# Attention's residual added by accumulating transfers, its bias by ScalarE; one more product in parts, and three jobs at other points of the slot

## The chip, the cores and the metric

The kernel runs on one core of one Trainium2 chip. The metric is the device time of one execution in microseconds (us). The core's engines are named as in the profile: PE (TensorE), DVE (VectorE), ACT (ScalarE), POOL (GpSimd, which also issues transfers) and SP (SyncE, which only issues transfers). Each engine works through its own queue in order.

## The reference

Two layers work on four images of 64 x 64 pixels with 256 channels. The first is full self-attention over the 4096 pixels of an image with a residual; the second is a depthwise 3 x 3 convolution ("perception"), two pointwise layers with a GELU, and a local attention over 3 x 3 windows.

```python
# layer 0, per image, N = 4096 pixels
q, k, v = x @ Wq + bq, x @ Wk + bk, x @ Wv + bv          # q, k: 32 wide; v: 256 wide
x = gamma * softmax(q @ k.T) @ v + x
# layer 1
perceived = depthwise_conv3x3(x, w_perc) + b_perc         # 256 -> 768 channels
hid = gelu(perceived @ w_up1 + b_up1)                     # 768 -> 512
h = x + hid @ w_up2 + b_up2                               # 512 -> 256
q, k, v = split(h @ w_qkv + b_qkv)
out = h + local_attention_3x3(q, k, v)
```

## The kernel before, in words

**Slots.** An image is cut into 8 blocks of 8 rows (512 pixels), so there are 32 slots (NSLOT). Slot s runs the attention of block s, and beside it the later work of earlier blocks: the perception of block s-2, the hidden layer, update, guide, scores and local values of block k = s-3, and the output of block a = s-5. The order of every engine is the order in which the program is written.

**Points.** A slot has 16 points. At point p, PE makes the energies of half group n = p+2 (two key tiles of 128 pixels; one tile `e` that all half groups share), the jobs of that point from the list `jobs`, and the weighted product of half group p (line 492). ACT turns `e` into the weights `p` by an exponential (line 434); there are three buffers of `p`. At the end of a slot stands DVE's summing up: the denominators (lines 528 to 562), and `evacuate` (line 579), which empties the four accumulators that the next slot's first product needs. At point 0 of the next slot `finish` scales the result (line 602).

**Products in parts.** A product in plain fp32 costs PE more than one whose operands were split into three parts (high, low, gap). ACT makes the high part (lines 439, 448), DVE the low and the gap (457/458 for one key tile, 522/532 for two). The even half groups are split whole. Of the odd ones only the second key tile is split, but both are in 9, 11 and 13 (`BOTH_IN_PARTS`). This is so in the "full" slots, which are all from 3 to 30 but 7, 15 and 23: 25 slots. `load_alone` (L346) loads the values' forms for this; the first tile's forms use the one buffer of `hid`.

**Denominators.** In a full slot the weights of half groups 0 to 13 (in the first slot of an image 2 to 13) are summed by transfers that POOL issues with accumulation (`sent<-p`, lines 509/511), and those of 14 and 15 by DVE. The send of half group n stands in the program at point n-1, ahead of that point's jobs. A buffer of `p` is free for half group n+3 only when the send of n has landed.

**The residual.** `xp` is a ring of four blocks of the input with a zero column on either side. `renew` loads a block at the start of its slot. `finish` adds attention's result and the bias to it by two DVE instructions (line 608), and `rim` (POOL) copies or clears the row that lies beyond the ring's end. Each block's perception reads one row of the block below: the taps with dy = 2, which are the 11th and later of its 54 DVE steps. `share` says how many steps stand behind each point.

**The jobs at the end of a slot.** `local_values` makes values of the local attention on PE (line 1036) and adds the bias on DVE (1048). `scores` has PE (1076), an exponential on ACT (1096) and a mask on POOL (1101). `local_sum` is eight POOL instructions (1120 to 1127; one more for a block on an image's edge). `border` is a short product (1017), an exponential and one or two POOL instructions. The two halves of `local_values` stand at points 10 and 13, the scores at 11 and 12, `local_sum` at 12 behind the second scores, `border` at 14.

Of the kernel before, what the change touches and what calls it, by code (L numbers as in the profile page):

```python
# [11 lines left out]
AF = mybir.ActivationFunctionType  # L12
ALU = mybir.AluOpType
# [4 lines left out]
B, H, W, C = 4, 64, 64, 256  # L18
N = H * W
CQK = C // 8  # L20
CH = C // P
HP, WP = H + 2, W + 2
NB = 512
RB = NB // W
# [15 lines left out]
NG = NT // GRP  # L40
SQ = 32
NJ = NB // SQ
NSLOT = B * NBLK
# [7 lines left out]
BELOW = 1.0 - 2.0**-13  # L51
IN_PARTS = (2, 4, 6, 8, 10, 12, 14)
ONE_IN_PARTS = (1, 3, 5, 7, 9, 11, 13, 15)
BOTH_IN_PARTS = (9, 11, 13)
BY_DMA = (3, 5, 7, 9, 11, 13)
BY_DMA_IF_FULL = tuple(range(14))

# [5 lines left out]
def attention_then_perception_kernel(  # L63
# [19 lines left out]
    nc = tc.nc  # L83
# [3 lines left out]
    def loaded(src, name, shape=None, queue=None):  # L87
        t = const.tile(list(shape or src.shape), F32, tag=name, name=name)
        (queue or nc.sync).dma_start(out=t, in_=src)
        return t  # L90
# [10 lines left out]
    def unshifted():  # L101
# [6 lines left out]
        def tile_of(shape, tag, name, bufs=1):  # L108
            return pool.tile(shape, F32, tag=tag, name=name, bufs=bufs)

        def bank(tag, name):
            return psum.tile([P, NB], F32, tag=tag, name=name, bufs=dict(m=2, acc=2 * CH)[tag])
# [14 lines left out]
        xv = xp.rearrange("p c (h w) -> p c h w", w=WP)  # L127

        def ring(slot):

            return 1 + slot % RING * RB
# [15 lines left out]
        for r in range(4):  # L147
            nc.scalar.dma_start(
                out=bqk2[r * CQK : (r + 1) * CQK, :], in_=b_qk[:, r % 2 : r % 2 + 1]
# [17 lines left out]
        for r in range(KR):  # L167
            m = near[r * KW : (r + 1) * KW]
            for half in range(2):

                for sign in (1, -1):
                    nc.gpsimd.affine_select(
                        out=m[:, half], in_=m[:, half], compare_op=ALU.is_ge, fill=0.0,
# [13 lines left out]
        for q in range(0, P, SQ):  # L187
            part = fold[q : q + SQ].rearrange("p (j r) -> p j r", r=SQ)
            nc.gpsimd.affine_select(
                out=part, in_=part, compare_op=ALU.not_equal, fill=1.0,  # L190
# [3 lines left out]
        def watch(values):  # L194

            n = values.free_size()
            for i in range(0, n, P):
                at = watched[:, : min(P, n - i)]
                nc.gpsimd.tensor_tensor(at, at, values[:, i : min(n, i + P)], ALU.add)
# [3 lines left out]
        def seen():  # L203

            i = next(free)
            return watched[:, i : i + 1]
# [15 lines left out]
        def full(s):  # L222
            return s > LAG_PERC and s % NBLK < NBLK - 1
# [7 lines left out]
        def alone(s, n):  # L231

            if last_one(s, n):
                return [1] * (n in ONE_IN_PARTS)
            return [i for i, ns in enumerate((BOTH_IN_PARTS, ONE_IN_PARTS)) if full(s) and n in ns]

# [116 lines left out]
        def project_v(s, pair, tag="m"):  # L353
# [10 lines left out]
            n = 2 * (s % NBLK) + pair  # L364
            split, one, both = (n in ns for ns in (IN_PARTS, ONE_IN_PARTS, BOTH_IN_PARTS))
            h = packed_h[:, s, bass.ts(pair, 2 * C)].rearrange("p (t c) -> p t c", c=C)
# [84 lines left out]
        def low_and_gap(s, n):  # L451
            for i in alone(s, n):
                high, (_, low, gap) = highs[s, n, i, P], rests.pop((s, n, i))
                if low is None:
                    low, gap = (tile_of([P, NB], "vs", f"o{x}_{s}_{n}", 4) for x in "lg")
                p = weights[s, n // 2, n % 2][:, i, :]
                nc.vector.tensor_tensor(low.bitcast(F32R), p, high, ALU.subtract)
                nc.vector.scalar_tensor_tensor(
                    gap.bitcast(F32R), low, -SPLIT, high, ALU.mult, ALU.add
                )  # L460
                lows[s, n, i, P], gaps[s, n, i, P] = low, gap
# [84 lines left out]
        def shared(s):  # L546

            a = s - LAG_ATT + 1
            return a if 0 <= a < DIRECT - 1 else None
# [15 lines left out]
        def on_all(values, turned, out, copy=nc.vector.tensor_copy):  # L565

            copy(
                squares(turned), values.unsqueeze(2).to_broadcast([P, NJ, SQ])
            )
            nc.vector.transpose(out, turned)  # L570

        def evacuate(s):
            acc = accs.pop(s)
            os = [tile_of([P, NB], "o", f"o_{s}_{c}", 2) for c in range(CH)]
            for o, gap in zip(os, acc[CH:]):
                nc.scalar.mul(o, gap, -1.0 / (SPLIT + 1.0))
            if in_two_sums(s):
                for c, o in enumerate(os):
                    nc.vector.tensor_tensor(o, acc[c], o, ALU.add)
                acc = os  # L580
            evacuated[s] = os, acc

        def finish(s, parts=((0, RB),)):

            n = NJ * (1 if shared(s) is None else 2)
            ps = bank("m", f"dps_{s}")[:, :n]
            given = parts_.pop(s).rearrange("p i j -> p (i j)")[:, :n]
            nc.tensor.matmul(ps, lhsT=fold, rhs=given, start=True, stop=True)
            inverse = tile_of([P, 2, NJ], "inverse", f"inverse_{s}")
            inverses[s] = inverse  # L590
            nc.vector.reciprocal(inverse.rearrange("p i j -> p (i j)")[:, :n], ps)

            rden = sums.pop(s)[:, 1, :]
            on_all(inverse[:, 0, :], turneds[s][:, 0, :], rden)
            watch(inverse.rearrange("p i j -> p (i j)")[:, :n])
            if s not in evacuated:
                evacuate(s)
            os, totals_ = evacuated.pop(s)
            for r0, r1 in parts:
                n = slice(r0 * W, r1 * W)  # L600
                for o, total in zip(os, totals_):
                    nc.vector.scalar_tensor_tensor(
                        o[:, n], total[:, n], gam_parts[:, 0:1], rden[:, n], ALU.mult, ALU.mult,
                        accum_out=seen(),
                    )
                for c, o in enumerate(os):
                    dst = xv[:, c, ring(s) + r0 : ring(s) + r1, 1 : 1 + W]
                    nc.vector.scalar_tensor_tensor(
                        dst, o[:, n].rearrange("p (h w) -> p h w", w=W), gbv[:, c : c + 1], dst,
                        ALU.add, ALU.add,  # L610
                    )
                if len(parts) > 1:
                    yield
            if s < NSLOT - 1:
                rim(s)
            yield

        def rim(s):


            g = s % NBLK
            if g == RING - 1:
                nc.gpsimd.tensor_copy(xv[:, :, 0, :], xv[:, :, RP - 2, :])
            elif g == NBLK - 1:
                nc.gpsimd.memset(xv[:, :, 0, :], 0.0)
            if g == RING:
                nc.gpsimd.tensor_copy(xv[:, :, RP - 1, :], xv[:, :, 1, :])
            elif (g == 0 and s > 0) or s == NSLOT - 2:
                nc.gpsimd.memset(xv[:, :, RP - 1, :], 0.0)
# [567 lines left out]
        def job(f, s, *args, n=NSLOT):  # L1197
            return [lambda: f(s, *args)] if 0 <= s < n else []
# [30 lines left out]
        for slot in range(NSLOT):  # L1229
            b, g = divmod(slot, NBLK)  # L1230
            if slot >= RING:
                renew(slot)
            k, a = slot - LAG_HID, slot - LAG_ATT
# [3 lines left out]
                job(hidden_part, k, 1, 0), job(hidden_part, k, 1, 1),  # L1237
                job(local_product, a, 0), job(local_product, a, 1),
                job(update, k, 0), job(update, k, 1), job(guide, k, 0),
                job(guide, k, 1), job(local_values, k, 0), job(scores, k, 0),  # L1240
                job(scores, k, 1) + job(local_sum, k - 1), job(local_values, k, 1),
                job(border, k), [],
            ]
            if slot in (1, 2):
                jobs[0] = [lambda: next(combine)] * 2
# [10 lines left out]
            n_steps, stepped = n_mixed, 0  # L1256


            share = [2, 6, 8, 4, 7, 2, 7, 4, 6, 4, 3, 1, 0, 0, 0, 0]
            if slot == LAG_PERC:  # L1260
                share = [4, 3, 6, 4, 5, 4, 5, 1, 5, 1, 5, 1, 5, 1, 4, 0]
            if slot == NSLOT - 1:
# [21 lines left out]
            for point in range(points):  # L1284
# [22 lines left out]
                    load_forms(*soon)  # L1307
                if point == 0:
                    low_and_gap(slot, 1)
                for do in jobs[point]:  # L1310
                    do()
                if slot and point == 0 and in_two_sums(slot - 1):
                    next(finish(slot - 1))
# [21 lines left out]
                if slot == 0 and point == 1:  # L1335
                    wb = const.tile([P, CH, MULT, TAPS + 1], F32, tag="wb", name="wb")
                    nc.gpsimd.dma_start(out=wb[:, :, :, :TAPS], in_=w_perc)
                    bias = loaded(b_perc, "bperc", queue=nc.gpsimd)
                    wperc, bperc = wb[:, :, :, :TAPS], wb[:, :, :, TAPS]
                    gam = loaded(gamma.partition_broadcast(P), "gam", [P, 1])  # L1340
                    gbv = loaded(b_v.rearrange("o (c p) -> p (o c)", p=P), "gbv")
# [33 lines left out]
            if in_two_sums(slot):  # L1375
                evacuate(slot)
            elif slot < NSLOT - 1:
                next(finish(slot))
# [17 lines left out]


        finishing = finish(last, ((0, 1), (1, RB)))
        next(finishing)
        run((guide, last - 2, 0, 0), (guide, last - 2, 1, 0))  # L1400
# [392 lines left out]
    with tc.manual_schedule():  # L1793
        wv, gam, wperc, bperc, wup1, bup1, wup2, bup2, blqk, blv = unshifted()
# [50 lines left out]
```

## Time and profile before

| | before |
|---|---|
| runs shown, median of 3 (lowest to highest) | 3191.09 us (3189.49 to 3192.02) |
| the profiled execution's own time | 3190.59 us |
| its span, first to last instruction | 3188.9 us |
| granted TensorE clock | 0.999 |
| PE busy | 3166.7 us, 99% |
| DVE busy | 2921.0 us, 92% |
| ACT busy | 1632.7 us, 51% |
| POOL busy | 745.4 us, 23% |
| DMA | 703.22 MB, 320504 packets |

Around the span lie 1.7 us. A "busy" PE may be waiting inside a matmul, since the ends of matmuls are modelled; starts are what the timeline is read by. Lines are named L and a number, tiles as in the program without their buffers' numbers, and `out<-in` says what an instruction writes and reads.

### The profile page before, as it was taken

Reading aid. Unit: us, or ns where it says so; the run is one execution under the profiler, and the core shown is the slowest. Engines: PE = TensorE matmul, PEld = TensorE weight load, DVE = VectorE, ACT = ScalarE, POOL = GpSimd, SP = SyncE. Lnnn points to the kernel's source line nnn. Section 1 sums busy time; section 2 is a strip of 40 time slices with the busy share of each in tenths; the row PEclk is TensorE's granted clock in tenths of the full one; section 3 lists DMA queues with packets and bytes.
Section 4 is the critical chain, followed back from the end, with each engine's and each line's share of the span. In section 5 each row is a group of like instructions: output and inputs, shape, how many; then the busy total and the mean of one; then the engine's idle time right before and its main releaser. Section 6 shows DMA issues by size and latency. Waiting matters only on the chain.

```text
span 3188.9 us, 39777 instructions
## 1 busy us (share of the span) xinstructions
PE 3166.7 (99%) x12652; PEld 2279.5 (71%) x12652; DVE 2921.0 (92%) x4264; ACT 1632.7 (51%) x2249; POOL 745.4 (23%) x1070
## 2 busy tenths in 40 slices
PE   9999999999999999999999999999999999999998
PEld 5557777766777777776777777777677777777755
DVE  5789999989999999998999999999899999999994
ACT  4445555555555555554555555554555555555432
POOL 4201122221222221222122222211221222222221
PEclk9999999999999999999999999999999999999999
DMA  8778888777888888877888888896788888888620
GB/s 269 227 206 220 231 225 232 226 235 230 228 232 244 238 223 241 227 205 249 239 223 234 225 243 236 229 239 194 260 232 232 223 232 228 240 238 239 165 51 28
DMA packets 320504, 703.22 MB, mean 221 GB/s; under 512 B 97233, under 2 KB 98273, under 8 KB 320161
## 3 DMA queue, kind: packets, MB, share of 16 engines
q1 hardware_dynamic: 246336, 448.01, 43.7%
q0 software_dynamic: 67280, 240.98, 34.2%
q10 hardware_dynamic: 6672, 11.60, 1.0%
q8 instruction: 105, 1.72, 0.2%
q14 instruction: 111, 0.90, 0.1%
HBM read 425.83 MB, written 79.82 MB: 159 GB/s over the span
## 4 chain that ended last, share of the span: by engine, by line
PE 90%; DVE 6%; issue 1%; DMA 1%; ACT 1%; SPq 0%; POOL 0%; ACTq 0%; DVEq 0%; POOLq 0%
PE acc L492 44%; PE e L429 7%; PE dx L872 6%; PE hid_gf L815 5%; PE hid_de L815 5%; PE hid_bc L815 5%; PE lv L1036 3%; PE lo L1169 3%; PE v L358 3%; PE g L967 3%; DVE perc L702 3%; PE s L1076 2%; PE hid_a L815 2%; PE qk L278 1%; PE hid L847 1%
## 5 line engine op out<-in xcount | busy, mean ns | idle before, releaser
L702 DVE SCALAR_TENSOR_TENSOR perc<-xp,wb,perc 128x526 f32<-128x526 f32 (+1 forms) x1356 | 937.5, 756 | 1.5 <-ACT perc L698 1.1
L434 ACT ACTIVATE p<-e 128x1024 f32<-128x1024 f32 x512 | 524.1, 1024 | 432.1 <-PE e L429 395.0
L511 POOL DMA_DIRECT2D sent<-p x316 | 267.9, 854 | 1385.3 <-ACT p L434 924.3
L492 PE MATMUL acc<-p,v 128*128 128x512 f32 x1268 | 583.7, 595 | 0.2 <-ACT v L374 0.2
L492 PEld LDWEIGHTS acc<-p,v 128*128 128x128 f32 x1268 | 235.7, 190 | 221.3 <-issue 211.6
L429 PE MATMUL e<-qa,ka 128*128 128x512 f32 x1024 | 351.4, 424 | 4.1 <-DMA ka<-st 1.3
L439 ACT ACTIVATE ph<-p 128x1024 fp32r<-128x1024 f32 x214 | 226.6, 1059 | 136.5 <-issue 64.2
L522 DVE TENSOR_TENSOR pl<-p,ph 128x1024 fp32r<-128x1024 f32 x214 | 266.5, 1245 | 16.8 <-ACT ph L439 16.8
L492 PE MATMUL acc<-ph,v 128*128 128x512 f32 x856 | 278.1, 446 | 0.7 <-DMA v<-packed_h 0.7
L532 DVE SCALAR_TENSOR_TENSOR pg<-pl,ph 128x1024 fp32r<-128x1024 f32 x214 | 265.8, 1242 | 12.6 <-DVE pl L522 0.5
L429 PEld LDWEIGHTS e<-qa,ka 128*128 128x128 f32 x1024 | 190.7, 188 | 80.0 <-issue 33.6
L492 PE MATMUL acc<-pl,vf 128*128 128x512 f32 x856 | 235.3, 397 | 0.0
L492 PE MATMUL acc<-pg,vf 128*128 128x512 f32 x856 | 230.0, 390 | 0.2 <-DVE pg L532 0.2
L872 PE MATMUL dx<-hid,wup 128*128 128x512 f32 x512 | 230.0, 592 | 0.0
L448 ACT ACTIVATE oh<-p 128x512 fp32r<-128x512 f32 x204 | 128.5, 630 | 189.0 <-PE acc L492 67.4
L492 PEld LDWEIGHTS acc<-ph,v 128*128 128x128 f32 x856 | 156.3, 188 | 54.3 <-issue 27.8
L492 PEld LDWEIGHTS acc<-pl,vf 128*128 128x128 f32 x856 | 161.2, 188 | 39.6
L492 PEld LDWEIGHTS acc<-pg,vf 128*128 128x128 f32 x856 | 160.6, 188 | 38.1 <-DVE pg L532 1.4
L838 ACT ACTIVATE hid<-hid,bup 128x512 f32<-128x512 f32 x120 | 80.2, 715 | 195.3 <-DVE hid L822 195.3
L492 PE MATMUL acc<-oh,v 128*128 128x512 f32 x408 | 178.7, 519 | 0.0
L708 DVE TENSOR_TENSOR perc<-perc 128x262 f32<-128x262 f32 x360 | 164.9, 472 | 6.3
L872 PEld LDWEIGHTS dx<-hid,wup 128*128 128x128 f32 x512 | 96.8, 189 | 98.6 <-issue 93.6
(232 smaller groups left out, 5629.9 us busy)
## 6 DMA issues: line engine op xcount, KB each, us to landing
sent<-p POOLq DMA_DIRECT2D x370, 512.0 KB, 6.7
vf<-packed_f SPq DMA_DIRECT2D x214, 512.0 KB, 5.9
v<-packed_h SPq DMA_DIRECT2D x204, 512.0 KB, 4.8
vo<-packed_o SPq DMA_DIRECT2D x279, 256.0 KB, 4.4
ka<-packed SPq DMA_DIRECT2D x1016, 64.0 KB, 3.6
xp<-in_x SPq DMA_DIRECT2D x30, 528.0 KB, 7.9
packed_f<-vlg POOLq DMA_DIRECT2D x28, 512.0 KB, 4.1
out<-lo SPq DMA_DIRECT2D x56, 256.0 KB, 4.0
```

The source lines that it names most:

```text
L429: nc.tensor.matmul(e[:, i, :], lhsT=keys[s, G][:, bass.ts(2 * half + i, P)].bitcast(F32R), rhs=queries[s].bitcast(F32R), start=True, stop= ...
L434: nc.scalar.activation(p, e, AF.Exp)
L439: nc.scalar.activation(high.bitcast(F32R), weights[s, G, half], AF.Identity, scale=BELOW)
L448: nc.scalar.activation(high.bitcast(F32R), p, AF.Identity, scale=BELOW)
L492: nc.tensor.matmul(accs[s][to + c], lhsT=w[:, bass.ts(c, P)].bitcast(kind), rhs=x.bitcast(kind), start=to not in started[s], stop=last,)
L511: nc.gpsimd.dma_start(out=sent[s, even], in_=p, accum_op=ALU.add)
L522: nc.vector.tensor_tensor(low.bitcast(F32R), p, high, ALU.subtract)
L532: nc.vector.scalar_tensor_tensor(gap.bitcast(F32R), low, -SPLIT, high, ALU.mult, ALU.add)
L702: nc.vector.scalar_tensor_tensor(acc, win, wt, acc, ALU.mult, ALU.add)
L708: nc.vector.tensor_tensor(t[:, to, :], t[:, a, :], t[:, b, :], op)
L815: nc.tensor.matmul(ps[:, n * C : (n + 1) * C], lhsT=w(j), rhs=rows_of(mixes[s, j][:, kind, :]), start=(j == 0), stop=(j == MULT - 1),)
L872: nc.tensor.matmul(ps, lhsT=wup2[:, d, bass.ts(c, P)], rhs=hids[s][:, d, :], start=(d == 0), stop=(d == NHC - 1),)
```

## The change

- Half group 15 joins `BOTH_IN_PARTS`: in the 25 full slots its first key tile is split into parts, too.
- For blocks 1 to 30 the result of attention is added to `xp` by two transfers with accumulation on POOL's queue (one for each half of the channels), in place of DVE's two instructions. The bias is added to the block ahead of that, at point 8 of its own slot, by two ACT instructions in place (`add_bias`).
- `rim` of the block before stands at point 1 behind that point's send, no longer in `finish`.
- Scores move from points 11 and 12 to 10 and 11, `local_sum` from 12 to 11, the local values from 10 and 13 to 12 and 14, and `border` from 14 to 13.
- Behind point 0 stand four steps of the perception in place of two; behind points 8 and 10 one less each.

```diff
-BOTH_IN_PARTS = (9, 11, 13)
+BOTH_IN_PARTS = (9, 11, 13, 15)
...
                 for c, o in enumerate(os):
                     dst = xv[:, c, ring(s) + r0 : ring(s) + r1, 1 : 1 + W]
+                    if 0 < s < NSLOT - 1:
+                        nc.gpsimd.dma_start(
+                            out=dst, in_=o.rearrange("p (h w) -> p h w", w=W), accum_op=ALU.add
+                        )
+                        continue
                     nc.vector.scalar_tensor_tensor(
...
-            if s < NSLOT - 1:
+            if s == 0:
                 rim(s)
             yield
+
+        def add_bias(s):
+            for c in range(CH):
+                dst = xv[:, c, ring(s) : ring(s) + RB, 1 : 1 + W]
+                nc.scalar.activation(dst, dst, AF.Identity, bias=gbv[:, c : c + 1])
...
-                job(guide, k, 1), job(local_values, k, 0), job(scores, k, 0),
-                job(scores, k, 1) + job(local_sum, k - 1), job(local_values, k, 1),
-                job(border, k), [],
+                job(guide, k, 1), job(scores, k, 0), job(scores, k, 1) + job(local_sum, k - 1),
+                job(local_values, k, 0), job(border, k), job(local_values, k, 1), [],
...
-            share = [2, 6, 8, 4, 7, 2, 7, 4, 6, 4, 3, 1, 0, 0, 0, 0]
+            share = [4, 6, 8, 4, 7, 2, 7, 4, 5, 4, 2, 1, 0, 0, 0, 0]
...
+                if point == 1 and slot > 1:
+                    rim(slot - 1)
+                if point == NG and 0 < slot < NSLOT - 1:
+                    add_bias(slot)
                 for do in jobs[point]:
                     do()
```

## The prediction

> **What bounds the kernel now.** I read the page first.
>
> ```profile
> PE 3166.7 (99%) x12652; PEld 2279.5 (71%) x12652; DVE 2921.0 (92%) x4264; ACT 1632.7 (51%) x2249; POOL 745.4 (23%) x1070
> ...
> PE 90%; DVE 6%; issue 1%; DMA 1%; ACT 1%; SPq 0%; POOL 0%; ACTq 0%; DVEq 0%; POOLq 0%
> ```
>
> PE sets the time; DVE is close behind, ACT and POOL are not. So a change is worth what it takes from PE's row of matmuls, less what it makes PE wait. I then read slot 13 (1202.0 to 1294.5), first in the chain in order of time (start, us):
>
> ```profile
> 1261.07 2.76 PE acc L492 x12
> ...
> 1270.60 2.92 PE acc L492 x12
> ...
> 1287.08 3.11 PE acc L492 x10
> ```
>
> A product with both key tiles in parts (x12) takes 2.76 to 2.79, with one (x10) 3.11. Next PE's and DVE's timelines at the slot's end (start, us):
>
> ```profile
> 1278.40 1.89 PE L1036 MATMUL lv<-wlv,h 128*128 128x256 f32 x8
> 1279.93 0.81 PE L492 MATMUL acc<-vo,v 128*128 128x512 f32 x2
> ...
> 1283.58 1.20 PE L492 MATMUL acc<-ph,v 128*128 128x512 f32 x4
> ...
> 1286.46 0.61 PE L429 MATMUL e<-qa,ka 128*128 128x512 f32 x2
> ...
> 1294.51 1.96 PE L492 MATMUL acc<-p,v 128*128 128x512 f32 x4
> ```
>
> ```profile
> 1280.54 0.68 DVE L1048 TENSOR_TENSOR lv<-lv,blv 128x512 f32<-128x512 f32 x1
> 1281.14 1.47 DVE L522 TENSOR_TENSOR pl<-p,ph 128x1024 fp32r<-128x1024 f32 x1
> ...
> 1283.84 0.72 DVE L457 TENSOR_TENSOR ol<-p,oh 128x512 fp32r<-128x512 f32 x1
> ...
> 1292.17 1.28 DVE L579 TENSOR_TENSOR o<-acc,o 128x512 f32<-128x512 f32 x2
> ```
>
> The product at 1294.51 is the next slot's first; it needs the first accumulator emptied, which DVE has done at 1292.17 + 0.68 = 1292.85. DVE is only 1.66 us ahead of PE here, after running from 1280.54 without a gap. This is the narrowest place of the slot. Last, POOL in the same stretch:
>
> ```profile
> 1271.22 0.96 POOL L1101 TENSOR_TENSOR lp<-lp,near 128x396 f32<-128x396 f32 x1 [4.74 <-ACT lp L1096]
> 1272.14 0.85 POOL L511 DMA_DIRECT2D sent<-p  x1
> 1275.96 1.22 POOL L1101 TENSOR_TENSOR lp<-lp,near 128x396 f32<-128x396 f32 x1 [2.97 <-ACT lp L1096]
> ...
> 1282.91 1.10 POOL L1127 TENSOR_TENSOR lsum<-lsum,pad 1x16 f32<-1x16 f32 x1
> ```
>
> The send of half group 13 goes out at 1272.14, just ahead of the 8.05 us (1275.96 to 1284.01) that the second mask and `local_sum` hold POOL.
>
> **The change part by part.** The sums are against the profiled execution's 3190.59, 0.5 below the median.
>
> *Half group 15 in parts.* The x10 product becomes x12: 3.11 - 2.78 = 0.33 us less PE, in 25 slots: -8.3. DVE gets one more low-and-gap pair at point 14; such a pair took 1.33 (1256.82 to 1258.15). ACT gets one more 128x512 high part, 0.63, where it idles 2 to 3 us between exponentials. The extra 256 KB load goes through `hid`'s buffer, free once PE is through the first half of product 13, 6 us ahead of use; such loads land in 4.4 (median). SP waits for that, but the load queued behind it waits for the end of the same product already. In 7, 15 and 23 the split of one block's values grows by 0.75 of DVE's time, under that place's lead of 0.8 to 1.3: nothing.
>
> *The residual.* 60 DVE instructions leave (1.42 a slot, 1205.70 to 1207.12) and two perception steps of 0.7 take their place at point 0; these are missing later, behind points 8 and 10. So DVE is where it was until point 7, 1.4 ahead by point 10, and level again after the new pair. The transfers must land before the 11th step, the first behind point 2, at 1220.83. The scaled result is there at 1205.1 and 1205.8; POOL needs some 1.2 an issue (estimate: 0.89 for the load below, 0.84 for an accumulating send, 0.58 for a plain one, so 0.26 for accumulating). The nearest rows for landing:
>
> ```profile
> sent<-p POOLq DMA_DIRECT2D x370, 512.0 KB, 6.7
> ...
> xc<-in_x POOLq DMA_DIRECT2D x4, 256.0 KB, 7.6
> ```
>
> The second has the same pieces of 64 elements; its longest took 8.3, a send's 9.5. With the last issue starting near 1206.4, and DVE up to 1.7 late (below), the second lands by 1217.6 at worst: hidden, 3 us to spare. In the four slots (as slot 13) where `rim` must copy a row of it first, POOL waits for the landing and copies in 0.77; still in time. Sends 2 and 3 queue behind, some 4 to 8 us later; their buffers are wanted by exponentials 5 and 6, at 1222 and 1232: covered. `add_bias` is 2 x 0.69 on ACT at point 8 (row L971); the exponential behind moves from 1259.39 to about 1260, the energies that wait for it come at 1263.8: covered. If that cover went, it would cost PE up to 1.4 a slot.
>
> The Trainium skill speaks against such pieces ("DMA: Bandwidth & Descriptors", Specifications): transfers under 512 B, these are of 256 B, run below line rate, with a read-modify-write. Its fit for POOL's queue (same page, Anatomy of one DMA) would give 2.6 us for 256 KB, and 7.6 was measured here; by either the sum gets nothing from the transfer.
>
> *The jobs moved.* Scores (1.34 on PE) for values (1.73) put PE 0.39 ahead in points 11 and 12; from point 15 the total is the same. Two things come of it.
>
> First, DVE. The second half of the values is now made at point 14, behind PE's energies 16, and product 14 begins where it did, 1283.58. The result is there 0.36 later (as 1278.40 + 1.89 against 1279.93), at 1283.94. DVE gets there about 1282 (1283.84, less 0.60 for the values that now come later and 1.4 for the steps that went) and must wait: an in-order queue, with the new pair, the denominators and `evacuate` behind. From 1283.94: values 0.60, new pair 1.33, then the old stretch from 1283.84 to 1292.85, 9.01: the accumulator is free at 1294.88. PE, 0.33 faster, wants it at 1294.18. So PE waits 0.7, with the semaphore 0.75 (an estimate; 0.04 to 0.1 lies between an end and a start in these timelines). Bounds: by the chain's merged ends (border's end 1283.65, dps's end 1294.67) it is 0.3; if the 0.2 by which product 14 was slow here (2.97) goes too, 0.95. I take 0.75, as starts are recorded and ends are not. Before, the lead was 1.6 to 2.1 in most full slots; in 8, 16 and 24 it was 0.55, since one more addition stands ahead of point 14's work, but this addition is now under the new wait. So 24 slots (4 to 30 without 7, 15, 23): +18.0. Slot 3 had 3.2.
>
> Second, POOL. `local_sum` is moved past send 13, which now follows it. The mask starts at 1271.22 - 0.39 = 1270.83, the send at 1278.88. It lands 7.0 later (two sends of this part of the slot: 6.8 and 7.1; early ones 4.6), at 1285.9. Only then is the buffer free for exponential 16, 1.03, so energies 17 come at 1287.0 instead of 1286.46: 0.55. Behind exponential 16 nothing of ACT is due before energies 17. That lies in the same PE stretch as the 0.75, and the larger counts. In seven slots (4, 11, 12, 19, 20, 27, 28) `local_sum` has a row or clears more and runs 0.3 to 1.4 longer: some 0.4 over the 0.75 each, with scatter +2. The ends: landing in 4.6 gives 0, in 9.5 gives 3.0 a slot.
>
> Sum: -8.3 + 18.0 + 2 = +11.7; 3190.6 + 11.7 = 3202.3, on the median 3203.
>
> **The rivals.**
>
> *The cover holds (faster).* DVE reaches the accumulator in time, PE keeps the 0.33: 3191 - 8 = 3183. For: PE waits for DVE nearly nowhere now, and the lead is 1.66. It decides where the stretch from the values to the accumulator is under 10.2 us instead of 10.94. Against: that stretch ran without a gap. Chance 0.17.
>
> *Half of it.* The wait is 0.3, by the chain's ends: 24 x 0.3 - 8.3 = -1, up to 0.55: 3190 to 3196. Chance 0.17.
>
> *The send is what counts.* With landings at 8 to 8.5 (some rows reach 9.5) PE waits 1.5 to 2 at energies 17: 24 x 1.5 - 8 = +28, and less if only some do: 3211 to 3222. Chance 0.12.
>
> *The transfers land late.* An accumulation in pieces takes over 14 us for the pair; DVE then stands at the 11th step, with all splits of points 2 and 3 behind it. DVE's idle time is about 2 a slot; each us more costs 27: 3225 and up. For: a piece is read, added and written. Chance 0.09.
>
> My own case, 0.45: 3197 to 3211.
>
> **How the numbers follow.** What a measurement of this kernel can tell from no change is 0.2%, 6.4 us: under 3184.7 is faster, over 3197.5 slower. Slower: 0.45 + 0.12 + 0.09 = 0.66; within: 0.17; faster: 0.17. The range reaches from the full gain, 3182, to the middle of the send's case, 3216; outside are the upper rivals' ends and a little below. My own case alone is 3197 to 3211.
>
> **What would show it.** Right: PE's busy sum falls by some 8 us in its matmuls, but a wait of 0.5 to 1 stands before the first product of each full slot (released by L579); DVE waits about 2 us for values at point 14, released by line 1036; exponential 16 waits for a send that starts near the end of `local_sum`; the 11th step has no wait. Wrong: no wait before that product, or an idle DVE at point 2 released by the transfers, or PE waiting at energies 17 for 2 us and more.

## The result and the profile after

| kernel | median (us) | ratio to the kernel before, 95% interval |
|---|---|---|
| before | 3191.12 (3189.49 to 3193.56, 8 runs) | |
| after | 3201.53 (3198.36 to 3202.99, 8 runs) | 1.0031 [1.0021, 1.0040] |

The change makes the kernel slower by 0.3%. The profiled execution of after took 3202.99, its span is 3201.2: 12.3 more than the span of before.

First the page: engine totals, shares of the chain that ended last, and two rows of the DMA issues (KB each, median us from issue to landing).

```profile
PE 3170.9 (99%) x12702; PEld 2286.0 (71%) x12702; DVE 2918.5 (91%) x4254; ACT 1680.4 (52%) x2334; POOL 858.8 (27%) x1130
...
PE 74%; DVE 14%; DMA 5%; issue 3%; SPq 2%; ACT 1%; POOL 0%; ACTq 0%; DVEq 0%
...
sent<-p POOLq DMA_DIRECT2D x370, 512.0 KB, 7.1
...
xp<-o POOLq DMA_DIRECT2D x60, 256.0 KB, 6.3
```

The chain has moved: PE had 90% of it and DVE 6%. Now 14% lie on DVE. PE's busy time did not fall by the 8 us that the split of half group 15 was to save: a matmul that waits counts as busy. Starts have to be read instead. This is the chain of after at the end of slot 13, in order of time (start us, us, what):

```profile
1297.86 1.31 DVE turned L559 x2
1299.18 0.02 issue
1299.20 1.23 DVE parts L562
1300.43 0.14 issue
1300.57 0.38 PE dps L588 x2
1300.95 3.52 PE acc L492 x8
```

PE's first work of the next slot's product, the small matmul `dps`, starts 0.14 after DVE has reduced `parts`. Here are DVE's and PE's timelines of the same stretch (start us, us, engine, line, operation; in brackets the idle time before it and what ended it).

```profile
1287.38 1.23 DVE L532 SCALAR_TENSOR_TENSOR pg<-pl,ph 128x1024 fp32r<-128x1024 f32 x1
1290.10 0.69 DVE L1058 TENSOR_TENSOR lv<-lv,blv 128x512 f32<-128x512 f32 x1 [1.50 <-PE lv L1046]
1290.71 0.68 DVE L457 TENSOR_TENSOR vo<-p,vo 128x512 fp32r<-128x512 f32 x1
...
1299.20 1.22 DVE L562 TENSOR_REDUCE parts<-turned 128x32 f32<-128x1024 f32 x1
1300.34 1.28 DVE L579 TENSOR_TENSOR o<-acc,o 128x512 f32<-128x512 f32 x2
```

```profile
1288.18 1.89 PE L1046 MATMUL lv<-wlv,h 128*128 128x256 f32 x8
1289.71 1.28 PE L492 MATMUL acc<-ph,v 128*128 128x512 f32 x4
...
1298.92 1.46 PE L825 MATMUL hid_bc<-perc,wmix 128*128 128x256 f32 x6
1300.57 0.38 PE L588 MATMUL dps<-parts,fold 128*128 128x32 f32 x2 [0.19 <-DVE parts L562]
1300.78 3.68 PE L492 MATMUL acc<-p,v 128*128 128x512 f32 x8
```

DVE stands idle for 1.50 until PE has made the second local values, then has 10.92 without a gap to the first accumulator (1290.10 to 1300.34 + 0.68), and PE waits for `parts` in the middle of that. The waits over the whole run (us in total, times, longest) say the same. The first line is of before, the others are of after:

```profile
PE dps L588 <- DVE parts L562: 2.2, 2, 1.4
...
PE dps L588 <- DVE parts L562: 7.4, 26, 1.5
...
DVE lv L1058 <- PE lv L1046: 42.8, 31, 3.6
```

**Where the 12.3 us lie.** Each half group's two energies matmuls (L429) mark the begin of a point. The table sums the time from one pair to the next over the 24 full slots 4 to 30, worked out from their starts in each trace. "Point 0" is the stretch with the wait above, "15" holds product 15, "11" product 11. "Ends" are slots 7, 15 and 23, "start" is all up to slot 4, "rest" slot 31 and after.

| kernel | point 0 | 11 | 15 | all 16 | ends | start | rest |
|---|---|---|---|---|---|---|---|
| before | 184.1 | 116.6 | 85.4 | 2223.6 | 395.2 | 326.9 | 243.1 |
| after | 193.2 | 118.6 | 76.2 | 2227.6 | 400.9 | 330.7 | 242.0 |
| e1_old_order | 188.0 | 109.7 | 76.2 | 2211.0 | 396.9 | 328.1 | 241.0 |
| e2_no_fifteen | 183.1 | 117.3 | 85.4 | 2223.9 | 397.8 | 327.7 | 241.1 |
| e3_order_only | 183.8 | 125.5 | 85.5 | 2233.7 | 395.3 | 328.0 | 243.9 |
| e4_fifteen_only | 189.0 | 115.1 | 76.2 | 2217.3 | 395.2 | 328.3 | 245.6 |
| e5_residual_only | 183.8 | 109.5 | 85.4 | 2216.1 | 396.7 | 328.5 | 241.0 |
| e6_values_back | 187.8 | 116.9 | 76.3 | 2218.5 | 397.2 | 329.2 | 241.3 |
| e7_sum_back | 193.3 | 118.5 | 76.2 | 2238.1 | 400.8 | 327.4 | 242.3 |
| e8_dve_at_end | 193.5 | 118.8 | 76.2 | 2229.0 | 396.5 | 327.9 | 243.8 |
| e9_values_late | 195.7 | 110.1 | 77.6 | 2223.1 | 400.7 | 328.7 | 242.0 |
| e10_mask_memset | 193.4 | 109.4 | 76.2 | 2218.3 | 400.6 | 329.7 | 241.4 |
| e11_best | 187.1 | 111.8 | 76.2 | 2212.5 | 395.2 | 329.1 | 242.7 |
| e12_best_first | 185.6 | 111.9 | 77.3 | 2211.8 | 395.2 | 329.1 | 242.6 |

Each row is one execution. That of after is the slowest of its eight, 1.5 above the median, and that of e5 is 3.8 under its median; so a row explains where time lies, and the medians say how much it is.

So the full slots account for 4.0 of the 12.3, slots 7, 15 and 23 for 5.7, the start for 3.8, and the rest gives back 1.2. Within the full slots point 0 (+9.1) and the shorter product 15 (-9.2) cancel. A slot's wait shows in point 0 of the slot behind it: 20 of the 24 waits are in the first column (8.4 of the 9.1), three are in "ends" (1.3, at point 0 of slots 7, 15 and 23) and one is in "rest" (0.4, slot 31), 10.1 in all. The other 0.7 of the column are in slots 8, 16 and 24, behind a slot that isn't full.

### The profile page after: what moved, and what is told of

The parts are those of the page before. It is cut to its first block, busy times and chain, and to the rows that moved or that the text cites. A ratio compares the mean times of both kernels' runs of the same rounds, so it can differ in the third digit from the quotient of the medians.

```text
span 3201.2 us, 40284 instructions
## 1 busy us (share of the span) xinstructions
PE 3170.9 (99%) x12702; PEld 2286.0 (71%) x12702; DVE 2918.5 (91%) x4254; ACT 1680.4 (52%) x2334; POOL 858.8 (27%) x1130
## 4 chain that ended last, share of the span: by engine, by line
PE 74%; DVE 14%; DMA 5%; issue 3%; SPq 2%; ACT 1%; POOL 0%; ACTq 0%; DVEq 0%
PE acc L492 35%; PE dx L882 6%; PE e L429 6%; PE hid_gf L825 4%; PE hid_de L825 4%; DVE perc L712 3%; PE v L358 3%; PE lo L1179 3%; PE g L977 3%; PE hid_bc L825 3%; PE lv L1046 2%; DVE den L540 2%; DMA vo<-packed_o 2%; DMA ka<-packed 2%; SPq L241 1%
## 5 line engine op out<-in xcount | busy, mean ns | idle before, releaser
L712 DVE SCALAR_TENSOR_TENSOR perc<-xp,wb,perc 128x526 f32<-128x526 f32 (+1 forms) x1356 | 958.1, 769 | 2.3 <-ACT perc L708 2.0
L511 POOL DMA_DIRECT2D sent<-p x316 | 296.1, 1012 | 1131.2 <-ACT p L434 774.8
L492 PE MATMUL acc<-p,v 128*128 128x512 f32 x1168 | 538.8, 597 | 0.2 <-ACT v L374 0.2
L492 PEld LDWEIGHTS acc<-p,v 128*128 128x128 f32 x1168 | 217.3, 190 | 208.4 <-issue 201.1
L429 PE MATMUL e<-qa,ka 128*128 128x512 f32 x1024 | 351.5, 424 | 3.5 <-DMA ka<-st 1.6
L532 DVE SCALAR_TENSOR_TENSOR pg<-pl,ph 128x1024 fp32r<-128x1024 f32 x214 | 265.1, 1239 | 14.1 <-PE acc L492 0.9
L429 PEld LDWEIGHTS e<-qa,ka 128*128 128x128 f32 x1024 | 189.8, 188 | 79.8 <-issue 36.1
L492 PE MATMUL acc<-oh,v 128*128 128x512 f32 x408 | 168.6, 494 | 0.0
```

The lines of the kernel that those rows point to most:

```text
L429: nc.tensor.matmul(e[:, i, :], lhsT=keys[s, G][:, bass.ts(2 * half + i, P)].bitcast(F32R), rhs=queries[s].bitcast(F32R), start=True, stop= ...
L492: nc.tensor.matmul(accs[s][to + c], lhsT=w[:, bass.ts(c, P)].bitcast(kind), rhs=x.bitcast(kind), start=to not in started[s], stop=last,)
L511: nc.gpsimd.dma_start(out=sent[s, even], in_=p, accum_op=ALU.add)
L532: nc.vector.scalar_tensor_tensor(gap.bitcast(F32R), low, -SPLIT, high, ALU.mult, ALU.add)
L712: nc.vector.scalar_tensor_tensor(acc, win, wt, acc, ALU.mult, ALU.add)
```

## The experiments

Three theories went in. **Chain theory**: the second local values at point 14 put DVE's stretch late, and PE waits for its end. **Send theory**: send 13 behind `local_sum` lands late. **Transfer theory**: the accumulating transfers land late. Each of the first eight runs undoes or does one part. All ratios are to the kernel before, run on the same chip; where two runs are compared by their medians, the chips may differ, and before's medians on them lie between 3190.5 and 3191.4.

**One part undone or done alone.** The whole change with the old order of jobs:

```diff
-                job(guide, k, 1), job(scores, k, 0), job(scores, k, 1) + job(local_sum, k - 1),
-                job(local_values, k, 0), job(border, k), job(local_values, k, 1), [],
+                job(guide, k, 1), job(local_values, k, 0), job(scores, k, 0),
+                job(scores, k, 1) + job(local_sum, k - 1), job(local_values, k, 1),
+                job(border, k), [],
```

> The changed kernel with the jobs at their old points (values 10 and 13, scores 11 and 12, local_sum at 12, border 14). Chain theory (DVE's stretch from the second values to the first accumulator holds PE at the next slot's first product): the second values are made at 13 and the stretch starts some 4.9 us of PE earlier; it then takes 0.60 + 2.70 + 1.33 + 9.01 = 13.64 us from 1280.3 in slot 13 and ends at 1294.0, where PE wants it at 1294.2: no wait, and the full gain of half group 15 stays, -8.3 against before, less what slots 7, 15 and 23 and the first three slots lost after the change (some 6): 3188 to 3191. Send theory (send 13 behind local_sum holds energies 17): the same time, since the send is ahead again. Transfer theory (the residual's transfers crowd the queues and the memory): nothing recovers, 3198 to 3202.

Measured 3179.23 (3176.88 to 3182.54), ratio 0.9964 [0.9950, 0.9977]: faster than every theory had it, 22 below after. The order is what makes the change slow; the transfers are not.

The whole change without half group 15:

```diff
-BOTH_IN_PARTS = (9, 11, 13, 15)
+BOTH_IN_PARTS = (9, 11, 13)
```

> The changed kernel without half group 15 in BOTH_IN_PARTS. Chain theory: the stretch behind the second values is shorter by the pair, 1.33, so it ends 0.9 ahead of PE; the wait of 0.42 at the first product goes, and so does the gain of 0.38 at point 15: about the same per slot as after, 3200 to 3203, with no wait before the first product and the DVE stretch near 9.6 us. Send theory: local_sum still ahead of send 13, so PE's wait stays and the gain goes: 3207 to 3211, with a wait at energies 17. Transfer theory: 3207 to 3210, since only the gain goes.

Measured 3193.87, ratio 1.0008 [0.9999, 1.0017]. Product 15 gives back its 9.2, but the wait at point 0 is gone altogether (183.1): without the new pair, 1.33 of DVE's time, DVE is ready before PE. In a regular slot the wait has a threshold, and the pair of half group 15 and the later values reach it only together. All three expectations were too high. The chain theory was right that wait and gain leave with each other; the other differences from after lie in the ends (3.1 less), at points 11 and 12 (2.4 less) and in the start (3.0 less, 1.7 of it the clock, see the last section).

The kernel before with the new order of jobs alone (the two lines of the first diff, the other way round):

> The kernel before with the new points of the jobs alone. Chain theory: DVE's stretch starts at 1283.94 and has no new pair, 0.60 + 9.01: it ends at 1293.55, 0.95 ahead of PE's first product: no wait there; only the 0.15 a slot at product 11 (the mask on POOL beside DVE) is left: 3191 to 3195. Send theory: the send lands 7 after 1278.9, PE waits 0.55 at energies 17 in 24 slots: 3203 to 3207. Transfer theory: no residual transfers, so 3191, as before.

Measured 3202.51, ratio 1.0036 [1.0023, 1.0050]. Point 0 shows no wait (183.8), so this cannot be the chain. The time is just under what the send theory asked for, but its wait stands in one slot only: 1.4 at energies 17 in slot 27. The loss is at point 11: 125.5, 8.9 over before, where the chain theory had 0.15 in each of 24 slots; see below.

The kernel before with half group 15 alone, and the change without both half group 15 and the new order, so that only the residual is left:

```diff
-BOTH_IN_PARTS = (9, 11, 13)
+BOTH_IN_PARTS = (9, 11, 13, 15)
```

> The kernel before with half group 15 in BOTH_IN_PARTS alone. Chain theory: the second values at 13; the lead of DVE at the first accumulator goes from 1.66 by 1.33 and 0.33 to about 0; DVE's idle time, some 2.1 a slot, goes to 0.5. Most of the gain of 8.3 stays: 3183 to 3188. If DVE as a whole becomes the bound (its 92% plus 33 us over 25 slots), part of it is lost: 3188 to 3192. Send theory and transfer theory: 3183, nothing they speak of is there.

Measured 3188.25, ratio 0.9990 [0.9981, 0.9999], at the upper end of what the chain theory had. Product 15 gives its 9.2, and point 0 takes 4.9 back, all of it in slots 8, 9, 16, 17, 24 and 25: in a regular slot PE doesn't wait (7.60).

> The residual by transfers with its bias, rim and steps alone: the changed kernel with BOTH_IN_PARTS and the jobs' points as before. Chain theory: nothing in the regular slots (DVE is level again, the transfers land 3 us and more ahead of the 11th step); what slots 7, 15, 23 lost after the change at point 1 (1.3 to 2.0 each, a projection that waits for an input load of 7.6 us issued after DVE) stays if the transfers make it: 3191 to 3196. Transfer theory: it carries the whole loss: 3199 to 3206. Send theory: 3191.

Measured 3187.92, ratio 0.9991 [0.9982, 1.0000], under all three expectations. Transfers and ACT's bias do not cost what the transfer theory gave them. If they gain anything (the interval ends at 1), it is at point 11 (109.5 against 116.6).

**Only the second local values back at point 13** (`border` at 14), the rest of the change kept:

```diff
-                job(local_values, k, 0), job(border, k), job(local_values, k, 1), [],
+                job(local_values, k, 0), job(local_values, k, 1), job(border, k), [],
```

> The changed kernel with the second local values at 13 and border at 14; scores at 10 and 11 and local_sum at 11, ahead of send 13, stay. Chain theory: the stretch starts some 3.6 us earlier, no wait at the first product, the gain stays but for product 11 and slots 7, 15, 23: 3191 to 3195. Send theory: send 13 is where it was in the changed kernel: 3199 to 3203. Transfer theory: 3199 to 3203.

Measured 3185.52, ratio 0.9984 [0.9975, 0.9993]: 16 less than after, from two jobs that change places, and more than the chain theory asked for. In the table 5.4 of it lie at point 0 and 3.7 at the ends, of which 1.3 are the waits there.

**`local_sum` behind send 13 again** (at point 12, one later than in the change):

```diff
-                job(guide, k, 1), job(scores, k, 0), job(scores, k, 1) + job(local_sum, k - 1),
-                job(local_values, k, 0), job(border, k), job(local_values, k, 1), [],
+                job(guide, k, 1), job(scores, k, 0), job(scores, k, 1),
+                job(local_values, k, 0) + job(local_sum, k - 1), job(border, k),
+                job(local_values, k, 1), [],
```

> The changed kernel with local_sum at 12, behind send 13; scores at 10 and 11, local values at 12 and 14 stay. Chain theory: nothing changes at the first product, 3199 to 3203. Send theory: the wait goes, 3189 to 3193. Transfer theory: 3199 to 3203.

Measured 3210.40, ratio 1.0059 [1.0045, 1.0072]: 9 slower than after, where none of the theories had a time above 3203. The send theory falls, with the sign turned round. The loss is at point 13, 97.6 against 87.2 in after. Two answers of the DMA view say why, both for the window 1278.6 to 1278.9 in slot 13 (issue, KB, us to landing), first of this run, then of after:

```profile
sent<-p POOLq DMA_DIRECT2D x1, 512.0 KB, 8.8
vo<-packed_o SPq DMA_DIRECT2D x1, 256.0 KB, 8.3
```

```profile
vo<-packed_o SPq DMA_DIRECT2D x1, 256.0 KB, 4.6
```

Send 13 is issued at 1277.90 here, 0.74 ahead of a 256 KB load of value forms that product 13 needs. The load lands at 1286.92, 8.3 after its issue, and PE loads these weights at 1287.03, after 0.52 of idle time. In after `local_sum` holds POOL from 1278 to 1284.87, the send leaves behind it, and the load lands in 4.6. Over the 24 full slots the load takes 8.2 in the median in e7 (6.6 to 9.4) and 6.0 in after (4.3 to 7.7). The work ahead of the send keeps a big transfer out of the way of a small one that is due sooner. In before most slots have the same lead of 0.74 and a load of 6.1 to 7.6, but there the second local values stand ahead of product 13 on PE, and nothing waits for it (point 13 takes 4.91 to 4.92 in every full slot).

**The residual on DVE in slots 6, 14, 22 and 30**, whose finish lies in the slot with the projections of the next image:

```diff
-                    if 0 < s < NSLOT - 1:
+                    if 0 < s < NSLOT - 1 and s % NBLK != NBLK - 2:
                         nc.gpsimd.dma_start(
...
-                if point == NG and 0 < slot < NSLOT - 1:
+                if point == NG and 0 < slot < NSLOT - 1 and g != NBLK - 2:
                     add_bias(slot)
```

> The changed kernel, but for blocks 6, 14, 22 and 30 the residual and bias are added by DVE again (no transfers at point 0 of slots 7, 15, 23 and 31, no bias by ACT in slots 6, 14, 22, 30). If the transfers make the projection of point 1 wait in slots 7, 15 and 23 (it waited 1.3 to 2.0 there), 3.5 to 5 us come back: 3196 to 3198. If the wait comes of DVE being late there (by the 0.4 of the wait at the first product, and now 1.42 more for the two instructions, less the two steps that have moved ahead, which stay: net 1.4 later), nothing comes back or it grows: 3201 to 3204.

Measured 3198.07, ratio 1.0022 [1.0013, 1.0031]; the ends are at 396.5 against 400.9. The chain of after in slot 7 shows what went away:

```profile
620.06 0.72 DVE lrden L570
...
620.80 0.37 SPq L267
621.17 0.04 issue
621.21 7.64 DMA xc<-in_x
628.86 0.04 issue
628.90 1.07 PE qk L278 x2
```

The projection of point 1 waits for a 256 KB load of the input. The same load lands in 4.07 in before and 4.52 in this run; in after the two accumulating transfers were issued at 614.56 and 615.55 and landed at 620.28 and 623.78, and the load, issued at 621.21, takes 7.64. It isn't DVE that is late: with the residual on DVE the load leaves 1.1 later in slot 7 than in after (counted from the slot's begin), and lands 2.0 earlier. Point 1 of these slots: 12.95 before, 14.1 to 14.9 in after, 12.95 here.

**The loss at point 11.** In after, e3 and before alike, product 11 waits for DVE's last piece of half group 11, `og` (L458). DVE's and POOL's timelines, in after:

```profile
1276.50 0.68 DVE L457 TENSOR_TENSOR ol<-p,oh 128x512 fp32r<-128x512 f32 x1
1277.21 1.34 DVE L458 SCALAR_TENSOR_TENSOR og<-ol,oh 128x512 fp32r<-128x512 f32 x1
```

```profile
1276.90 1.10 POOL L1111 TENSOR_TENSOR lp<-lp,near 128x396 f32<-128x396 f32 x1 [2.55 <-ACT lp L1106]
```

An instruction that takes 0.69 elsewhere takes 1.34 while POOL's mask of the local scores runs beside it. In before, beside the mask at 1271.22:

```profile
1271.36 1.37 DVE L458 SCALAR_TENSOR_TENSOR og<-ol,oh 128x512 fp32r<-128x512 f32 x1
```

To test this, the mask was replaced by a `memset` of the same tile, which leaves the masking out:

```diff
-                nc.gpsimd.tensor_tensor(pv, pv, mask, ALU.mult)
+                nc.gpsimd.memset(pv, 1.0)
```

> The changed kernel with GpSimd's masking of the local scores replaced by a memset of the same tile, so the masked exponentials are left out. Collision theory (a GpSimd operation that reads SBUF beside it takes VectorE's gap of half group 11 from 0.69 to 1.34 us): that operation is back at about 0.7, point 11 loses its 0.15 us in 24 slots and up to 6 more where values come late, so 3193 to 3198. If the operation is slow for another reason: it stays at 1.3 and the time at 3200 to 3203.

Measured 3190.76, ratio 1.0000 [0.9991, 1.0009]: 11 less than after. DVE in this run:

```profile
1272.94 0.69 DVE L458 SCALAR_TENSOR_TENSOR og<-ol,oh 128x512 fp32r<-128x512 f32 x1
```

```profile
1273.31 0.43 POOL L1111 MEMSET lp<- 128x396 f32 x1 [3.33 <-ACT lp L1106]
```

Point 11 is at 109.4, near the 108.7 of 24 undisturbed ones of 4.53. The gain is more than expected: a regular point 11 went from 4.86 to 4.54, 0.32 and not 0.15 (the expectation had counted from the 4.71 of before, which has the same loss in it), and slots 22 and 29, where two of DVE's instructions meet the mask in after (1.49 and 0.89, point 11 at 5.64), are at 4.54 too.

The slowing is gone, but this run alone does not tell a `memset` from a mask: without the first mask, beside which three steps of the perception took 2.82 and not 2.12, DVE is earlier, and `og` now starts ahead of POOL's instruction. In e1 it starts ahead as well, of a real mask:

```profile
1268.63 0.69 DVE L458 SCALAR_TENSOR_TENSOR og<-ol,oh 128x512 fp32r<-128x512 f32 x1
```

```profile
1268.83 1.33 POOL L1111 TENSOR_TENSOR lp<-lp,near 128x396 f32<-128x396 f32 x1 [4.73 <-ACT lp L1106]
```

So what decides is which of the two starts first. All the traces of this case together say it without exception. Where the mask was first (198 cases), `og` took 1.33 to 1.50 and ended 0.54 to 0.56 behind the mask; where `og` was first (118 cases), it took 0.69 and the mask ended 0.81 to 0.83 behind it. That a `memset` ahead would not hold DVE up rests on three cases (0.68 to 0.69 beside the `memset` of `lsum`). The Trainium skill has this as a rule ("SBUF — State Buffer", 🔬 SBUF: two separate sides): a VectorE operation with two SBUF inputs and a GpSimd operation that reads SBUF need the same pair of ports, and the one that starts first holds it for its whole instruction. The two groups of cases agree with it.

In a regular slot the kernel before loses 0.18 at point 11 by this, at most 4.3 in 24 slots. The other 3.6 of its 7.9 (116.6 against 108.7) are in slots where the next energies wait for a load of keys (`ka`) that lands late; in slot 27 it lands at 5.12 after the point's begin, and the energies start at 5.26. e3, without the 1.4 that the residual's removal saves DVE, loses 0.68 in a regular slot, 16.8 in all. e1 and e5, with the scores at their old points and DVE 1.4 earlier, have `og` ahead of the mask and lose 1.

**The two halves of the order apart.** Scores and first values at their old points, `border` and the second values as in the change:

```diff
-                job(guide, k, 1), job(scores, k, 0), job(scores, k, 1) + job(local_sum, k - 1),
-                job(local_values, k, 0), job(border, k), job(local_values, k, 1), [],
+                job(guide, k, 1), job(local_values, k, 0), job(scores, k, 0),
+                job(scores, k, 1) + job(local_sum, k - 1), job(border, k), job(local_values, k, 1), [],
```

> The changed kernel with the scores and the first local values back at points 11, 12 and 10 and only the border (13) and the second local values (14) as the change puts them. Against the run with the old order (3179.2). Chain theory: the end of the slot pays its 0.42 us again in 24 slots, so 3188 to 3191, and product 11 keeps no wait for VectorE. Load theory (a send of 512 KB issued ahead of local_sum holds up the 256 KB load of key forms that product 13 needs): with the 1.28 us of the second local values gone from point 13, that product also waits about 0.4 us, 10 more: 3197 to 3201. If neither holds: 3179 to 3182.

Measured 3197.83 (3194.58 to 3199.59), ratio 1.0022 [1.0013, 1.0031]. Point 11 keeps no loss (110.1) and point 0 pays (195.7), as the chain theory has it, but the time is at the load theory's figure. That theory is not the reason: point 13 is as in after (87.3), because send 13 goes out at 1277.12, practically with the two loads of value forms (1276.67 and 1277.16), which land in 3.4 and 3.9. Where the send has a lead, as the 0.74 in e7, the load is held up, and not where both leave together; in slots 10 and 16 of e9 itself the send has that lead, and the second load takes 7.4 and 7.0, against 3.6 to 6.0 in the other full slots. The waits are some 9.4 over e1 (7.7 at point 0, 1.3 in the ends, 0.4 in slot 31), near the 10.1 that the chain theory had. What it missed lies at points 13 to 15 (3.5) and at point 1 of the ends (2.2); the cause of the 3.5 is open.

**A faster version.** e1 already beats both kernels; e8's edit was added to it, then the split of half group 15's first key tile was left out in the first slot of an image:

> The old order of jobs with the rest of the change, and the residual done on VectorE in slots 6, 14, 22 and 30. Transfer theory for slots 7, 15 and 23 (the accumulating transfers stand in the way of the input load that point 1's projection waits for): point 1 there is back at 12.95 from 13.5 to 13.7, 1.9 less than 3179.2: 3176 to 3178. If point 1 waits for VectorE instead, 3179 to 3181.

Measured 3180.18 (3177.11 to 3181.15), ratio 0.9964 [0.9951, 0.9978]. The ends come back (395.2, point 1 at 12.94), but 2.1 is lost at point 11, to late loads of keys in slots 4, 11, 24 and 26. It can't be told from e1.

```diff
-            return [i for i, ns in enumerate((BOTH_IN_PARTS, ONE_IN_PARTS)) if full(s) and n in ns]
+            return [i for i, ns in enumerate((BOTH_IN_PARTS, ONE_IN_PARTS)) if full(s) and n in ns
+                    and not (n == 15 and i == 0 and s % NBLK == 0)]
```

> The run before this one, with half group 15's first key tile in parts left out in slots 8, 16 and 24. Chain theory: the starts of slots 9, 17 and 25 come back from 8.1 to 8.3 to 7.6 (1.8 less), point 15 of slots 8, 16 and 24 gives back 0.39 each (1.2 more): 0.6 less in all, within what can be told apart. If the start of these slots waits for something else, they stay at 8.1 to 8.3 and the time is 1.2 more.

Measured 3178.59 (3175.19 to 3180.45), ratio 0.9958 [0.9944, 0.9971]. The starts of slots 9, 17 and 25 are back at 7.60 to 7.61 from 8.1 to 8.3, as the chain theory has it: in an image's first slot the new pair alone reaches the threshold. This is the lowest median, 0.4% under before, though not to be told from e1 and e11.

## Why the prediction was right, and where not

**The direction was right, and so was the mechanism of the wait.** The order of jobs, through the second local values at point 14, turns a gain into a loss. e1, e6 and e9 show it. DVE's idle time ahead of these values was put at about 2, it is 1.50; the stretch was put at 10.94, it is 10.92.

**The term of 18.0 was mis-sized by half, by one step: who waits for what.** The prediction, as the description of the kernel ahead of it, let the next slot's first product wait for the first accumulator (L579). In the trace this product starts at 1300.78, before that instruction ends (1301.02), and so it is in every full slot of after. It can't be writing the accumulators that DVE reads then; that it takes over the banks of the other two, which ACT emptied at 1296.93, is likely, but the trace does not name banks. What waits is `dps`, for `parts`. These are the two in before:

```profile
1291.04 1.22 DVE L562 TENSOR_REDUCE parts<-turned 128x32 f32<-128x1024 f32 x1
```

```profile
1294.37 0.30 PE L588 MATMUL dps<-parts,fold 128*128 128x32 f32 x2
```

With the prediction's own numbers this gives the right size: `parts` ended at 1291.04 + 1.22 = 1292.26 in before, 2.03 later is 1294.29, and PE wants it at 1294.37 - 0.33 = 1294.04; with the 0.14 of the chain, 0.39. Point 0 of a regular slot went from 7.61 to 8.03: 0.42. So 24 x 0.42 = 10.1, not 18.0, and all of it is in the table.

**Product 15** was put at 0.33, it is 0.38 (3.56 to 3.18): 9.6 in the 25 slots, not 8.3.

**Send 13 (+2) cost nothing.** It landed 4.6 after its issue at 1284.81 (4.5 to 5.5 in all full slots), not 7.0. Exponential 16 did wait for it, as forecast, but ended at 1290.49, 2.2 ahead of energies 17 at 1292.69. e7 shows that its later place is even worth 9. The prediction weighed the send only as one who comes late, not as one who stands in the way of a load.

**Half group 11 was not in the prediction.** The trace of before had the 1.37 beside 0.69, and with it a loss of up to 4.3 that the change could have removed. The prediction had DVE "1.4 ahead by point 10", but asked what this is worth only at the slot's end.

**"The transfers are hidden"** holds for the 11th step, which shows no wait, though POOL needs 3.19 for the two issues (rows of 1.61 and 2.20 that overlap), not 1.2 each. It does not hold where another transfer is close to being late: point 1 of slots 7, 15 and 23 was put at nothing and costs 4.5, and e8 brings it back.

**The start** cost 3.8. Of this 1.7 lie ahead of slot 0's work, a stretch that takes from 25.4 to 27.4 over the runs and 27.2 and 27.3 in e3 and e4, which have no transfers of the residual; its cause is open. Another 1.7 are the clock of the last section.

**The total** came out close largely by chance. The priced terms were +11.7; the trace has +0.5 for them, and with its own terms rightly sized the sum would have said no change: 10.1 for the waits, -9.6 for product 15, nothing for the send. In their place came 11.8 that the prediction had at nothing: 4.5 at point 1 of slots 7, 15 and 23, 4.7 in the full slots (2.0 of it at point 11), 4.2 at the start, less 1.6 in the rest. The price of the step that was blamed stands better: with the second local values at point 14, the time is 16 higher (after against e6) or 18.6 higher (e9 against e1), where 18 was foretold; but only some 7 to 9 of it is the wait.

Of the rivals, "half of it" had the better wait (0.3), and its time of 3190 to 3196 lacked the same terms; "the send is what counts" and "the transfers land late" are refuted as mechanisms for a full slot.

Two readings to be careful with. A fall of PE's busy sum by some 8 was named as a sign of being right, and it rose by 4.2 with 50 matmuls more. And in this trace the chain of waits counts loads of value forms (`vo<-packed_o`) as links to DVE's split, which start within 0.01 of their landing: DVE was busy with the local values until then (1290.10 + 0.69), and in e1 the same split starts at 1280.88, ahead of the landing at 1281.90. So the 5% of DMA and a part of the 14% of DVE are not to be taken as waits of PE.

## What to carry to other kernels

Before you price a late engine, find the first instruction that takes its result, in the trace: here it is `dps`, which wants `parts`, and not the product, which the code's reader takes to want the accumulator; with that the wait is 0.42, and not the estimated 0.75. A transfer that is itself hidden still costs, if a load with little lead is issued behind it: list what each queue sends in the few microseconds after. And when a change is a bundle, run its parts apart: here two of three gain a little alone, together they gain 0.4%, and the third takes more than that away.

## What the runs showed of the hardware

- **The clock.** Slot 2's first point took 7.89 in some runs (before, e2, e3, e4, e7, e8) and 9.59 in the others, with the same work in it. The windows view of after (us, then busy time of PE, PEld, DVE, ACT, POOL, then PE's granted clock, DMA share and GB/s):

```profile
178.00:179.00 1.00, 1.00 (x4) 0.66 (x5) 0.79 (x4) 0.00 (x0) 0.26 (x1) 0.74 0.05 16
179.00:180.00 1.00, 1.00 (x2) 0.38 (x2) 0.93 (x3) 0.00 (x0) 0.14 (x1) 0.50 0.00 0
180.00:181.00 1.00, 1.00 (x2) 0.34 (x1) 1.00 (x3) 0.00 (x0) 0.00 (x0) 0.50 0.00 0
181.00:182.00 1.00, 1.00 (x2) 0.34 (x1) 0.97 (x3) 0.00 (x0) 0.44 (x1) 0.55 0.00 0
```

  The clock is at half for about 3.4 us, worked out as (0.26 + 0.50 + 0.50 + 0.45) x 2, and 1.7 us are lost. It follows 2 us of 20 matmuls with one column each (`small`). The Trainium skill ("TensorE: Matmul & The Clock Gate", Part 1: The HAM clock gate) has the clock set by activity in a free-running window of 3413 ns; that would explain both the length and why runs with the same work at this point differ. No run here changed these matmuls, so their part in it is not shown.
- **DVE beside POOL**: `og` took 0.69 when it started ahead of POOL's mask and 1.33 to 1.50 when it started behind it. The one that came second ended a fixed time after the first: 0.54 to 0.56 for `og`, 0.81 to 0.83 for the mask.
- **Landing times depend on what is issued just ahead**: a 256 KB load of value forms took 8.2 in the median with a 512 KB send issued 0.7 ahead of it (e7) and 6.0 without one (after), the input load 4.1 or 7.6, and a 512 KB send 4.6 in a quiet stretch and 8.8 among loads.
- **An accumulating transfer of 256 KB in pieces of 256 B** landed in 6.3 (median of 60); of a pair issued 1.0 apart in slot 13's finish the first took 5.5, the second 7.3. POOL's rows for the issue are 1.6 to 2.2 long.
